# A norm without its subtraction, and two matmul groups moved by a slot, in a Mamba-and-attention kernel

## The chip, the cores and the metric

The kernel runs on one core of one Trainium2 chip. The metric is the device time of one execution in microseconds (us). Five engines matter: TensorE (PE, with its weight loads as PEld), VectorE (DVE), ScalarE (ACT), GpSimd (POOL) and SyncE (SP), whose queue issues nearly all DMAs. [...]

## The reference

The input x is 4 images of 512 channels and 64 x 64 positions (4096 positions in sequence). Two layers follow each other. `_gn` is a group norm over groups of 16 channels.

```python
def layer_norm(x, g, b):
    mu = jnp.mean(x, axis=-1, keepdims=True)
    var = jnp.mean((x - mu) ** 2, axis=-1, keepdims=True)
    return (x - mu) * lax.rsqrt(var + EPS) * g + b
...
def step(h, inp):                       # inside mamba()
    dt_t, B_t, C_t, x_t = inp
    dA = jnp.exp(dt_t[:, :, None] * A)
    h = dA * h + (dt_t * x_t)[:, :, None] * B_t[:, None, :]
    y = jnp.einsum('bds,bs->bd', h, C_t)
    return (h, y)
...
# layer 0, _L0_conv_ref
xn = layer_norm(xf, norm_g, norm_b)
chunks = xn.reshape(B, L, 4, D_MODEL).transpose(2, 0, 1, 3).reshape(4 * B, L, D_MODEL)
ym = mamba(chunks, in_proj_w, conv_w, conv_b, x_proj_w, dt_proj_w, dt_proj_b, A_log, D_param, out_proj_w)
ym = ym + skip_scale * chunks
y = ym.reshape(4, B, L, D_MODEL).transpose(1, 2, 0, 3).reshape(B, L, C)
y = layer_norm(y, norm_g, norm_b)
y = jnp.einsum('blc,oc->blo', y, proj_w) + proj_b
...
x = x + _L0_conv_ref(_gn(x), ...)       # layer 0
x = x + _L1_conv_ref(_gn(x), ...)       # layer 1: linear attention over the 4096 positions
```

`mamba` works on 128 channels with 256 inner channels and 16 states: an input projection, a causal convolution of 4 taps, Silu, projections to dt, B and C, softplus, the scan above, a gate by Silu(z) and an output projection.

## The kernel before, in words

Everything lies with channels on the partitions (128) and positions along the free axis. A tile is 512 positions of an image (32 tiles), a step is one chunk of 128 channels of a tile (c = 0 to 3, 128 steps), and a step is cut into 16 slots (`SLOTS`). A slot (`slot`, from L657) scans two times 128 rows x 512 positions, a row being a channel and a state: GpSimd makes `bx` = dt x B two slots ahead (`drive`, L655), ScalarE makes `dA` by Exp into PSUM three scans ahead (`decay`, L647), VectorE scans (L673). A product with C on VectorE follows (`product`, L696): it covers 384 of the 512 positions and reads C from PSUM, where a matmul `c_all` (`c_row`) has spread it; GpSimd takes the other 128 positions (L684). TensorE then sums the states into `y` (`fold_states`). `c_all` has a single PSUM buffer, holds C for two slots, and is emitted when the product of a pair's second slot has been emitted. The products usually come one slot late, in the middle of the next slot; after the slots in `AWAY = (3, 10)` this is changed, so that slots 4 and 11 hold two products with one scan between them and slots 5 and 12 hold none.

Around the scan, the rest of the work is emitted slot by slot by `after()`. Some of it has fixed slots:

- `take_y` (ScalarE) and `gate` (GpSimd, L720) at slots 0/8 and 1/9;
- `time_banks` (two matmuls `pt`) at slot 2, `time_steps` (two Softplus, each way a table load) at slot 3;
- `inputs`, the input projection and convolution of the step after next, as `front`: four pieces of two tap matmuls into `pc`, two matmuls `pz`, one piece at each of the slots 3, 5, 6, 7, 8, 9;
- `out_proj` (four small matmuls with `skd`, two with `w_op`, into `po`) of the step before at slot 4, `with_skip` (a ScalarE copy) at slot 6, after which `leave` is added if the step was a tile's last;
- `to_rows` (GpSimd's dt product L561, two DMAs) at slot 4, Silu (with two table loads) at slot 10, `mixers` (`pd`) from slot 12.

The rest comes from four queues of generators: `ahead` (the next tile's load, group norm and layer norm: `normed`), `late` (the finished tile's second layer norm and projection: `projected`, matmuls `pp`), `rest` (the attention of the previous image: `pq`, `pk`, `pr`) and `light` (the next image's statistics). A generator yields words for what may come next: "wide" for a VectorE instruction over 4 x 512 positions, "one ahead" and "two ahead" for the matmuls that prepare it, "free" and "more" for what may go at once. `may` says at which slots such a word is allowed; `limit` says how many PSUM work banks (3 in all) the queues may hold; `credit` is a budget of TensorE work per slot. `later(n, ...)` emits something n slots later.

A layer norm (`layer_norm`, L363) sums over channels with matmuls (`mu_sums`), copies the sums (L373), spreads the mean into a bank (`mu`), subtracts it from the tile with a wide VectorE instruction (L390), squares on ScalarE (L396), does the same again for the variance (`var_sums`, `var`), takes Ln and Exp (L403, L404) and multiplies with a second wide instruction (L410). Names with `_a` are the norm of `normed`, with `_b` that of `projected`.

Of the kernel before, what the change touches and what calls it, by code (L numbers as in the profile page):

```python
# [14 lines left out]
P = 128  # L15
T = 512
# [8 lines left out]
def kernel(  # L25
# [143 lines left out]
    for i in range(NC):  # L169
        nc.vector.memset(mean[i * LANE : i * LANE + 1, :], 1.0 / C)  # L170
    grp = const.tile([P, P // GROUP, GROUP], F32, tag="grp", name="grp")
    nc.gpsimd.memset(grp, 1.0 / GROUP)
# [133 lines left out]
    for c in range(NC):  # L306
        nc.vector.tensor_scalar(w_pr[:, c, :], w_pr[:, c, :], g_sb[:, c : c + 1], None, ALU.mult)


    def stats_tile(name):  # L310
# [47 lines left out]

    def layer_norm(v, name, gained):


        def means(parts, what, when):
            yield from room()  # L363
            sums = work_bank(f"{what}_sums_{name}")
            for c in range(NC):
                mm(
                    sums[c * LANE : (c + 1) * LANE, :], ones.to_broadcast([P, LANE]), parts[c],
                    start=True, stop=True, abreast=NC,
                )
            got = wk.tile([P, T], F32, tag="sq", name=f"{what}_got_{name}", bufs=4)  # L370

            def take():
                nc.scalar.copy(got, sums)  # L373
                free()

            copied = later(1, take)
            yield
            yield from until(copied)
            yield when
            yield from room(when)  # L380
            bank = work_bank(f"{what}_{name}")
            mm(bank, mean.to_broadcast([P, P]), got, start=True, stop=True)
            return bank

        while norming:
            yield "wait"
        norming.append(name)
        mu = yield from means([v[:, c, :] for c in range(NC)], "mu", "one ahead")
        yield "wide"
        nc.vector.tensor_tensor(v, v, bc(mu, NC), ALU.subtract)  # L390
        free()
        yield "free"
        sqs = []
        for c in range(NC):
            sqs.append(wk.tile([P, T], F32, tag="sq", name=f"sq_{name}_{c}", bufs=4))
            nc.scalar.activation(sqs[c], v[:, c, :], AF.Square)  # L396
            if c == 1:
                yield "free"
        var = yield from means(sqs, "var", "two ahead")
        rs = wk.tile([P, T], F32, tag="sq", name=f"rs_{name}", bufs=4)  # L400

        def root():
            nc.scalar.activation(rs, var, AF.Ln, bias=eps)  # L403
            nc.scalar.activation(var, rs, AF.Exp, scale=-0.5)  # L404

        rooted = later(1, root)
        yield
        yield from until(rooted)
        yield "wide"
        nc.vector.tensor_tensor(v, v, bc(var, NC), ALU.mult)  # L410
        free()
        norming.clear()
        yield
        if gained:
            for c in range(NC):
                nc.scalar.activation(
                    v[:, c, :], v[:, c, :], AF.Identity,
                    bias=b_sb[:, c : c + 1], scale=g_sb[:, c : c + 1],
                )
                if c % 2:  # L420
                    yield "free"

    def normed(xn, pad, prev_pad, b, t, norm):
# [9 lines left out]
        yield from group_norm(body, body, norm)  # L433
        yield from layer_norm(body, f"a_{b}_{t}", True)
        nc.gpsimd.tensor_copy(pad, xn[:, :, T : T + NTAP - 1])

    def projected(ym, stats, x1, b, t):

        nm = f"{b}_{t}"
        yield from layer_norm(ym, f"b_{nm}", False)  # L440
        while no_tile():
# [8 lines left out]
        for o in range(NC):  # L450
            yield from room()
            pp = work_bank(f"pp_{nm}_{o}")
            for c in range(NC):
# [4 lines left out]
                if c == 1:  # L458
                    yield "more"
            taken.append(later(1, lambda o=o, pp=pp: take(o, pp)))  # L460
            yield
# [571 lines left out]
    with tc.manual_schedule():  # L1033
        credit, seen, mix, held[0], held_x[0] = 0.0, work["mm"], iter(()), 0, 0
        for n, (b, t, c) in enumerate(steps):
# [10 lines left out]
            for s in range(SLOTS):  # L1046
                def after():
# [17 lines left out]
                    if s == 3 and nxt is not None:  # L1065
                        nc.scalar.preload_act_table_set("softplus")
                        time_steps(nxt, names[n + 1])
                        nc.scalar.preload_act_table_set("natural_log_exp_and_others")
                    if s == 6 and before is not None:
                        pb_, pt_, pc_ = steps[n - 1]  # L1070
                        with_skip(before, xn[pb_, pt_], pc_)
                        if pc_ == NC - 1:
                            add_to(late, leave(pb_, pt_))
                    if s in (3, 5, 6, 7, 8, 9):
                        next(front, None)
                    if s == 4 and nxt is not None:
                        to_rows(nxt, 0, names[n + 1])
                        to_rows(nxt, 1, names[n + 1])
                    if s == 4 and before is not None:
                        pb_, pt_, pc_ = steps[n - 1]  # L1080
                        out_proj(before, xn[pb_, pt_], pc_, names[n - 1])
# [7 lines left out]
                    if s >= 12:  # L1089
                        next(mix, None)  # L1090
                    may = [
                        what for k, what in ((0, "wide"), (1, "one ahead"), (2, "two ahead"))
                        if any(a - 2 * k <= s <= a - k for a in AWAY) or (k == 2 and s == SLOTS - 1)
                    ]
                    if light and light[0][1] == "wait" or s in AWAY and not any(
                        q and q[0][1] == "wide" for q in (ahead, late)
                    ):
                        one(light)

                    limit[0] = 1 if 0 < s < 6 else 2  # L1100
                    credit = min(credit + 3.5 - (work["mm"] - seen), 2.6)
                    busy = False
# [75 lines left out]
```

## Time and profile before

| | us |
|---|---|
| median of 3 executions | 8081.14 |
| lowest, highest | 8077.04, 8089.07 |
| profiled execution, its own time | 8087.92 |
| its span in the profile | 8086.2 |
| first scan starts, last scan ends | 120.3, 7611.9 |
| DVE, POOL, PE, ACT busy | 7113.0, 6890.3, 6471.4, 5514.5 |

The page is of one execution. Busy time is the sum over an engine's instructions; PE's is that of pipelined matmuls, and an fp32 matmul appears as two records. A line number is that of the kernel's source; all matmuls have the helper's line L124 and are told apart by the names of what they write and read (out<-in, buffer numbers left out). In lines of waits come the total in us, the number of times and the longest one.

### The profile page before, as it was taken

The numbers are of one execution on the slowest core, as the hardware profiler recorded it, in microseconds if no ns is written. First come the engines' busy times: TensorE is split into PE (matmuls) and PEld (weight loads), VectorE is DVE, ScalarE is ACT, GpSimd is POOL, SyncE is SP. The second block draws the span as 40 slices with busy tenths as digits, with TensorE's granted clock in tenths as the row PEclk, the third lists the DMA queues.
The fourth block names the chain that finished last, engine by engine and source line by source line (L and its number), as shares of the span: only waits on it lengthen the run. The fifth ranks groups of instructions, "written<-read, shape, count | busy, mean of one in ns | idle before, by whom it ended". The sixth has DMA issues, their size and how long they took to land.

```text
span 8086.2 us, 92449 instructions
## 1 busy us (share of the span) xinstructions
PE 6471.4 (80%) x24800; PEld 2115.5 (26%) x24800; DVE 7113.0 (88%) x6815; ACT 5514.5 (68%) x8289; POOL 6890.3 (85%) x4597
## 2 busy tenths in 40 slices
PE   5677777667788878888788888888788888888599
PEld 1111111112222222322222222332222222322144
DVE  5999999999999999899999999999999999998600
ACT  4667777777767777677776767667777777776421
POOL 4999999999989989899998989888999999889600
PEclk8787888788899989898899999899889999999699
DMA  5666666666666666676666666667666666676402
GB/s 160 166 166 160 156 147 153 157 157 166 167 167 156 162 153 156 168 188 176 169 155 164 166 165 155 155 171 187 163 158 160 156 157 152 150 194 176 110 32 89
DMA packets 829199, 1265.98 MB, mean 157 GB/s; under 512 B 183912, under 2 KB 317560, under 8 KB 816384
## 3 DMA queue, kind: packets, MB, share of 16 engines
q1 hardware_dynamic: 804736, 1222.32, 59.7%
q0 software_dynamic: 16896, 33.56, 2.4%
q10 hardware_dynamic: 7040, 4.20, 0.2%
q8 instruction: 194, 3.18, 0.2%
q14 instruction: 333, 2.73, 0.1%
HBM read 1052.78 MB, written 206.57 MB: 156 GB/s over the span
## 4 chain that ended last, share of the span: by engine, by line
DVE 22%; PE 19%; DMA 17%; POOL 14%; issue 10%; ACT 9%; SPq 8%; POOLq 0%; DVEq 0%; ACTq 0%
DVE h L673 14%; POOL bx L655 10%; DMA d_all<-d_rows 9%; DVE h L696 7%; PE pq L124 5%; SPq L622 5%; DMA b_all<-b_rows 4%; ACT dA L647 3%; PE pc L124 3%; PE pr L124 3%; SPq L572 3%; PE y L124 3%; POOL h L684 2%; PE pp L124 1%; DMA c_sb<-c_rows 1%
## 5 line engine op out<-in xcount | busy, mean ns | idle before, releaser
L655 POOL TENSOR_TENSOR bx<-d_all,b_all 128x1024 f32<-128x1024 f32 x2048 | 4817.4, 2371 | 66.9 <-DVE h L673 51.5
L673 DVE TENSOR_TENSOR_SCAN h<-dA,st,bx 128x512 f32<-128x512 f32 x3584 | 4420.5, 1267 | 80.6 <-ACT dA L647 75.4
L647 ACT ACTIVATE dA<-d_all,a_t 128x512 f32<-128x512 f32 x4096 | 2780.4, 688 | 1764.2 <-DVE h L673 1727.5
L696 DVE TENSOR_TENSOR h<-h,c_all 128x768 f32<-128x768 f32 x2048 | 1906.7, 931 | 307.5 <-PE c_all L124 298.2
L124 PE MATMUL y<-h,fold 128*32 128x512 f32 x8192 | 1280.6, 701 | 160.5 <-POOL h L684 156.1
L684 POOL TENSOR_TENSOR h<-h,c_sb 128x512 f32<-128x512 f32 x1024 | 1299.3, 1269 | 121.4 <-DMA c_sb<-c_rows 33.5
L124 PE MATMUL pc<-xn,w_cv 128*128 128x512 f32 x2048 | 1078.8, 662 | 178.2 <-DVE xn L410 116.7
L124 PE MATMUL c_all<-parts,sel 128*128 128x384 bf16 x1024 | 368.3, 360 | 1058.5 <-DVE h L696 1056.1
L124 PE MATMUL pq<-w_qk,xa 128*128 128x512 f32 x2048 | 990.7, 615 | 1.9 <-ACT xa L348 1.9
L673 DVE TENSOR_TENSOR_SCAN h<-dA,bx 128x512 f32<-128x512 f32 x512 | 601.2, 1206 | 58.8 <-ACT dA L647 54.6
L124 PEld LDWEIGHTS pc<-xn,w_cv 128*128 128x128 f32 x2048 | 395.9, 204 | 807.7 <-issue 445.6
L124 PEld LDWEIGHTS <-sel 128*128 128x128 bf16 x1280 | 127.5, 100 | 1724.4 <-DVE h L696 1495.6
L683 POOL COPY st<-h 128x4 f32<-128x4 f32 x1024 | 206.9, 202 | 425.2 <-DVE h L673 382.2
L124 PEld LDWEIGHTS pq<-w_qk,xa 128*128 128x128 f32 x2048 | 402.8, 199 | 468.7 <-issue 446.2
L124 PE MATMUL pr<-xb,m 128*128 128x512 f32 x1024 | 500.4, 626 | 24.8 <-DMA xb<-x 16.5
L124 PE MATMUL pp<-xn,w_pr 128*128 128x512 f32 x1024 | 487.6, 602 | 3.8 <-DVE xn L410 3.8
L124 PEld LDWEIGHTS y<-h,fold 128*32 128x32 f32 x8192 | 170.9, 114 | 743.6 <-issue 281.0
L124 PE MATMUL y<-xz,dg 32*32 32x512 f32 x2048 | 340.4, 741 | 0.0
L720 POOL TENSOR_TENSOR xz<-xz 128x512 f32<-128x512 f32 x256 | 325.4, 1271 | 2.7 <-ACT xz L717 2.7
L561 POOL TENSOR_TENSOR dt<-dt,xz 128x1024 f32<-128x1024 f32 x128 | 302.2, 2361 | 25.5 <-ACT dt L553 25.5
L124 PE MATMUL pd<-xz,w_xp 128*128 128x512 f32 x512 | 311.6, 740 | 7.8 <-ACT xz L987 7.8
L771 ACT ACTIVATE kq<-pq 128x512 f32<-128x512 f32 x256 | 150.6, 588 | 232.6 <-PE pq L124 230.5
(169 smaller groups left out, 6063.9 us busy)
## 6 DMA issues: line engine op xcount, KB each, us to landing
d_all<-d_rows SPq DMA_DIRECT2D x2048, 256.0 KB, 6.6
b_all<-b_rows SPq DMA_DIRECT2D x4096, 64.0 KB, 2.2
d_rows<-dt SPq DMA_DIRECT2D x256, 512.0 KB, 3.7
c_sb<-c_rows SPq DMA_DIRECT2D x4096, 16.0 KB, 1.9
xs<-in_x_dram SPq DMA_DIRECT2D x32, 1024.0 KB, 5.8
xn<-in_x_dram SPq DMA_DIRECT2D x32, 1024.0 KB, 5.7
xr<-in_x_dram POOLq DMA_DIRECT2D x32, 1024.0 KB, 11.2
x<-xr SPq DMA_DIRECT2D x32, 1024.0 KB, 4.3
```

What stands on the lines that cost most here:

```text
L124: nc.tensor.matmul(out_, lhsT, rhs, **how)
L561: nc.gpsimd.tensor_tensor(f["both"][:, 1], f["both"][:, 0], f["xz"][:, 0], ALU.mult)
L572: nc.sync.dma_start(d[k * BLK : (k + 1) * BLK, v], src)
L622: nc.sync.dma_start(dst[k * BLK : (k + 1) * BLK, :], rows_[q * KS + k, :].partition_broadcast(BLK))
L647: nc.scalar.activation(dAs[k], fs[n]["d_all", e][:, 0, j, :], AF.Exp, scale=a_t[:, e, j, q : q + 1])
L655: nc.gpsimd.tensor_tensor(bxs[g], fs[n]["d_all", e][:, 1, jj * 2 : jj * 2 + 2, :], bc(b_all[g // JJ], 2), ALU.mult)
L673: nc.vector.tensor_tensor_scan(h[:, j, :], dAs.pop(2 * g + i), bxs[g][:, i, :], 0.0 if t == 0 else st[:, c, e, q, j : j + 1], ALU.mult, AL ...
L683: nc.gpsimd.tensor_copy(st[:, c, e, q, :], h[:, :, T - 1])
L684: nc.gpsimd.tensor_tensor(h[:, :, CUT:], h[:, :, CUT:], bc(c_sb.pop(g // JJ), NJ), ALU.mult)
L696: nc.vector.tensor_tensor(own, own, bc(c_all[g // JJ], 2), ALU.mult)
L720: nc.gpsimd.tensor_tensor(f["xz"][:, 1, e, :], f["xz"][:, 1, e, :], f["xz"][:, 0, e, :], ALU.mult)
L771: nc.scalar.activation(qk[i], pq, AF.Relu)
```

## The change

The second layer norm (`_b`, in `projected`) no longer subtracts the mean. The columns of the projection's weights, already multiplied by the gain, are made to have mean zero over the input channels at the start, so the projection takes the mean out of its input by itself. The variance is computed as the mean of squares minus the squared mean: a ScalarE Square of the mean bank, and one more matmul with `minus_first` that accumulates into the variance's bank. Both squares are taken about `about`, a constant from the skip scale and the mean of the norm's bias. The first norm keeps its form. `out_proj` moves from slot 4 to slot 3, `with_skip` and `leave` from 6 to 5, the first convolution piece from slot 3 to slot 4. The words "wide", "one ahead" and "two ahead" count from slot 10 only; statistics may come at slot 3 always; `limit` is 0 in slots 1 to 3, 1 in slots 0 and 4, 2 from slot 5 on (before: 1 in slots 1 to 5, otherwise 2); the credit grows by 3.6 instead of 3.5 a slot. Copies of sums and of the projection's result come by `soon()`, which is two slots later in slots 5 to 11.

```diff
+    minus_first = const.tile([P, 1], F32, tag="minus_first", name="minus_first")
+    nc.vector.memset(minus_first, 0.0)
+    nc.vector.memset(minus_first[0:1, :], -1.0)
...
+    pw = work_bank("pw_mean")
+    for c in range(NC):
+        mm(pw, ones.to_broadcast([P, P]), w_pr[:, c, :], start=(c == 0), stop=(c == NC - 1))
+    for c in range(NC):
+        nc.vector.scalar_tensor_tensor(
+            w_pr[:, c, :], pw, -1.0 / C, w_pr[:, c, :], ALU.mult, ALU.add
+        )
+    pw = work_bank("pw_about")
...
+    about = const.tile([P, 1], F32, tag="about", name="about")
+    nc.vector.scalar_tensor_tensor(about, pw[:, 0:1], -1.0 / C, sk, ALU.mult, ALU.mult)
...
+    def layer_scale(v, name):
...
+        yield from room()
+        sums = work_bank(f"mu_sums_{name}")
+        sums_into(sums, [v[:, c, :] for c in range(NC)], range(NC))
+        mu = yield from mean_of(sums, f"mu_{name}", None)
+        mu2 = wk.tile([P, T], F32, tag="sq", name=f"mu2_{name}", bufs=4)
+
+        def square():
+            nc.scalar.activation(mu2, mu, AF.Square, bias=about)
+            free()
+
+        squared = later(soon(), square)
...
+        def part(c):
+            sqs[c] = wk.tile([P, T], F32, tag="sq", name=f"sq_{name}_{c}", bufs=4)
+            nc.scalar.activation(sqs[c], v[:, c, :], AF.Square, bias=about)
...
+        var = yield from mean_of(sums, f"var_{name}", "two ahead", False)
+        mm(var, minus_first.to_broadcast([P, P]), mu2, start=False, stop=True)
+        yield from over_deviation(v, var, name)
...
     def projected(ym, stats, x1, b, t):
...
-        yield from layer_norm(ym, f"b_{nm}", False)
+        yield from layer_scale(ym, f"b_{nm}")
...
-            taken.append(later(1, lambda o=o, pp=pp: take(o, pp)))
+            taken.append(later(soon(), lambda o=o, pp=pp: take(o, pp)))
...
-                    if s == 6 and before is not None:
+                    if s == 5 and before is not None:
...
-                    if s in (3, 5, 6, 7, 8, 9):
+                    if s in (4, 5, 6, 7, 8, 9):
                         next(front, None)
...
-                    if s == 4 and before is not None:
+                    if s == 3 and before is not None:
                         pb_, pt_, pc_ = steps[n - 1]
                         out_proj(before, xn[pb_, pt_], pc_, names[n - 1])
...
-                        if any(a - 2 * k <= s <= a - k for a in AWAY) or (k == 2 and s == SLOTS - 1)
+                        if AWAY[1] - 2 * k <= s <= AWAY[1] - k
...
-                    if light and light[0][1] == "wait" or s in AWAY and not any(
+                    if light and light[0][1] == "wait" or s == AWAY[0] or s == AWAY[1] and not any(
                         q and q[0][1] == "wide" for q in (ahead, late)
...
-                    limit[0] = 1 if 0 < s < 6 else 2
-                    credit = min(credit + 3.5 - (work["mm"] - seen), 2.6)
+                    limit[0] = 0 if 0 < s < 4 else 1 if s in (0, 4) else 2
+                    credit = min(credit + 3.6 - (work["mm"] - seen), 2.6)
```

`sums_into`, `mean_of` and `over_deviation` hold what was inside `layer_norm`, and both norms call them.

## The prediction

> **What bounds the kernel now.** I read the page first, then each batch's stretch in the view of busy times by window, then DVE's waits, then the timelines of DVE and PE around one of those waits. The page gives the ranking, with DVE ahead of POOL:
>
> ```profile
> PE 6471.4 (80%) x24800; PEld 2115.5 (26%) x24800; DVE 7113.0 (88%) x6815; ACT 5514.5 (68%) x8289; POOL 6890.3 (85%) x4597
> DVE  5999999999999999899999999999999999998600
> ```
>
> The slot loop runs from the first scan at 120.3 us to the last at 7611.9 us. In windows cut at the batches (32 steps each), then the end after the loop:
>
> ```profile
> core 0: us, PE busy (x) PEld busy (x) DVE busy (x) ACT busy (x) POOL busy (x), PEclk, DMA share, GB/s
> 120.30:1920.60 1800.30, 1267.01 (x4666) 340.57 (x4666) 1744.36 (x1620) 1286.09 (x1905) 1711.50 (x1141) 0.81 0.66 159
> 1920.60:3823.00 1902.40, 1584.95 (x6192) 523.45 (x6192) 1777.10 (x1695) 1374.12 (x2072) 1724.19 (x1148) 0.91 0.66 166
> 7611.90:8086.20 474.30, 435.61 (x1508) 199.20 (x1508) 26.29 (x74) 102.80 (x166) 5.59 (x6) 0.92 0.17 58
> ```
>
> Batch 0 leaves DVE idle for 56 us of 1800; each later batch, which carries the attention of the one before, for 122 to 139 of 1890 to 1902. Together DVE stands idle for about 442 us of the loop's 7491.5. DVE's waits name the causes:
>
> ```profile
> DVE h L696 <- PE c_all L124: 298.2, 165, 6.0
> DVE kq L778 <- PE pk L124: 242.4, 42, 7.6
> DVE h L673 <- ACT dA L647: 130.1, 64, 46.7
> ```
>
> The kq wait lies almost wholly after the loop (9.8 us inside it) and 46.7 us of the dA wait before the first scan. Counting scans in the DVE timeline (two to a slot) sorts the rest: of the c_all wait 208 us fall in slot 4, 52 in slot 7, 18 in slot 15, 11 in slot 9; of the dA wait 62 in slot 12 and 19 in slot 5. The slot-4 wait in step 41, on DVE and then PE:
>
> ```profile
> 2458.61 2.25 DVE L410 TENSOR_TENSOR xn<-xn,var_a 128x2048 f32<-128x2048 f32 x1
> 2460.79 1.27 DVE L673 TENSOR_TENSOR_SCAN h<-dA,st,bx 128x512 f32<-128x512 f32 x1
> 2461.98 0.92 DVE L696 TENSOR_TENSOR h<-h,c_all 128x768 f32<-128x768 f32 x1
> 2462.83 1.27 DVE L673 TENSOR_TENSOR_SCAN h<-dA,st,bx 128x512 f32<-128x512 f32 x1
> 2465.73 0.95 DVE L696 TENSOR_TENSOR h<-h,c_all 128x768 f32<-128x768 f32 x1 [1.63 <-PE c_all L124]
> ```
>
> ```profile
> 2456.59 1.41 PE L124 MATMUL pt<-dt,w_dt 32*128 32x512 f32 x4
> 2460.92 2.47 PE L124 MATMUL pc<-xn,w_cv 128*128 128x512 f32 x4 [2.92 <-DVE xn L410]
> 2463.32 1.94 PE L124 MATMUL mu_sums_b<-xn,ones 128*32 128x512 f32 x8
> 2465.19 0.50 PE L124 MATMUL c_all<-parts,sel 128*128 128x384 bf16 x1
> ```
>
> In slot 4 the second product follows the first after one scan, so the c_all between them has 1.2 us. PE comes late: the slot-3 taps (pc) got the bank that the variance still held, waited 2.92 us for the wide multiply on DVE, and c_all stood behind them.
>
> **What the Trainium skill says.** (1) "PSUM — Partial Sum Buffer", Engine vs sequencer instructions: matmuls start and complete in program order. The fence above agrees: c_all's product input was ready at 2462.9, it started at 2465.19. (2) "VectorE: DVE Perf Modes", The perf-mode tier table: an fp32 tensor_tensor of 2048 columns takes 2293 ns, with a PSUM operand no faster. The trace has 2267 for L390. (3) "ScalarE: Activation LUTs", What ACT_TABLE_LOAD costs: a load is about 1283 ns, and a pointer bias adds 93 ns to an activation. The trace has 1283, and 614 for the Square without bias.
>
> **The change, part by part.** A matmul record costs PE 0.44 us in a row (the chain of waits ends with 256 pr records in 112.69 us); an fp32 matmul is two records. The instruction orders of both programs give counts and slots.
>
> *Subtraction removed.* 32 wide L390 instructions on mu_b at 2.267 us: 31 in the loop, one after it. DVE is the bound, and nothing hides them: 31 x 2.267 = **-70**.
>
> *Added for it.* ACT: 32 Squares of the mean (about 0.71 us with bias) and 93 ns more on each of 128 squares, 35 us on an engine idle 28% of the loop; it counts only in slots 3 and 10, where the order puts only a handful of them. PE: one more matmul a tile, 0.88 us in slots 5 to 7, counted with c_all below. Setup: four matmuls (3.5 us), four DVE passes of 512 columns (0.67 each by the bn_stats row L739, 2.7 in all) and the tiny *about*. DVE waits for x there, but the passes stand ahead of bn_stats that free x's buffers: between 0 and 6; **+2**. After the loop a 2.27 us pass gives way to a Square (0.71) and a matmul (0.88): **-1**, between -2 and +1.
>
> *Moves.* Slot 3 now emits out_proj, slot 4 the first taps; no new bank is taken in slots 1 to 3; wide steps stand at slot 10 (and var_a at slot 7) instead of 3 and 10. None of the moved steps issues a DMA; SP's and POOL's instructions and counts stay. Between the c_all of slots 2 and 4, PE's list shrinks to y (1.06 + 1.07 by the timeline), pt (1.41) and po (1.06 + 4 x 0.44): 6.4 us in every step, where before it held taps and often another 1 to 4 us, plus the wait for the bank. From the end of slot 1's product to slot 4's second DVE needs five scans (1.18 apart) and two products (0.85): 7.6 us. c_all itself takes 0.4. 6.8 against 7.6: the wait goes, but with only 0.8 to spare. po waits for gate on POOL, which ends about 2.9 us into slot 2, while PE reaches po's second half after 6: hidden. I leave 15 of the 208: **-193**.
>
> What is late next. Slots 4 and 5 now hold both tap pieces (3.5 us) and the background matmuls banned from slots 1 to 3. PE has about 8.6 us there (7.8 before, since c_all was late); 23 steps hold 9 us or more. Summing the excess, and scaling by what the same sum gave of slot 7's wait before (40 for 52): 33, **-19**. Slot 9: two steps reach 12, 11 becomes 15, **+4**. Slots 12 and 13 hold about 9.6 us in some 20 steps, where 8 to 9 was usual: 18 becomes 48, **+30**.
>
> ACT next. After slot 3's second scan it does dA, a table load, two Softplus, a table load, dA: 0.69 + 1.28 + 1.27 + 1.28 + 0.69, ready at 5.3 us. DVE without wide step or wait needs that dA at 5.4. Today's slot-4 wait hides anything more. In the fourth of steps with two group_norm pieces (0.80 each) ACT is ready at 6.7 to 6.9: 31 instead of 19, **+12**. At slot 10, Silu and loads make it 6.5; steps without a wide step wait 1.0. Steps c = 1 lose their cover and c = 2 gain it: **+5**.
>
> POOL next: bx was waited for 7 us. POOL is busy for 1712 to 1724 us a batch, and slot 4 gives it the dt product (2.36) besides. Between 0 and 60; the wait in slot 4 was its rest too: **+18**.
>
> Sum: -70 + 2 - 1 - 193 - 19 + 4 + 30 + 12 + 5 + 18 = **-212**. The profiled execution took 8087.9 (span 8086.2 and 1.7 around it), so 7876 on that scale; the median of the runs, 8081.1, is 6.8 lower: **7869**.
>
> **Rivals.** *The wait moves to ACT.* If nearly every step's dA in slot 5 comes 1.3 us late (two extra activations each time) then 166 instead of 31: **8004**. For it: ACT's 5.3 stands a hair below DVE's 5.4. Against: slot 3 is now empty of other activations in three steps of four. *POOL becomes the bound.* With the batches at 1800 us, as batch 0 with POOL 95% busy, the loop would be 7200: **7789**, hence no worse; but if half the dt product came onto the path in every step (128 x 1.18 = 151), **8002**. bx was ready 2 us or more ahead in most slots, which speaks against. *The bank ban bunches PE's work, and it ends slower.* The attention's matmuls come four to a bank, 3.5 us. If a bank's worth falls ahead of c_all(6) or c_all(14) and wholly on the path in four steps of five, 0.8 x 128 x 3.5 = 358 is lost: 8081 - 212 + 358 = **8227**. It decides from 1.7 us lost a step (212/128). For it: 86 of the steps pass 7 us in slots 4 and 5, where 68 did. Against: only 23 pass 9. *Larger gain*: if slots 9, 15 and bx don't grow and slot 7 vanishes, another 85: **7784**. That the subtraction only seems to go I exclude: the order holds no such instruction on mu_b.
>
> **Numbers.** The main case 0.68, its own range 7805 to 7935; the larger gain 0.09; ACT or POOL taking more of it 0.15; bunching to a slower kernel 0.06, to no change 0.02. No change means within 0.2%, 16 us, about what this measurement can tell. Range 7785 to 7985. Faster 0.92, same 0.02, slower 0.06.
>
> **What would show it.** DVE's busy time falls by about 72; no L390-like row on mu_b. The c_all wait falls from 298 to about 120, almost none of it in slot 4 and the most in slots 15 and 7. No pc waits for DVE's wide multiply. The dA wait stays near 145 in all. Batches 1 to 3 fall to about 1840 us, batch 0 to about 1770; the end stays at 474. Wrong would be: a slot-4 wait that survives, a dA wait above 250, a bx wait above 80, or an end longer by an attention left over (the order says none is).

## The result and the profile after

The changed kernel takes **8140.6 us** (median of 4 executions, 8134.4 to 8152.4) against 8083.1 (8077.0 to 8089.1) for the kernel before, run beside it: a ratio of 1.0073, interval 1.0055 to 1.0090. It is slower, where the forecast was 7869 and at most 7985. The profiled execution took 8134.4 (span 8132.7). In its page, the rows of engines and of slices that were shown of before:

```profile
PE 6532.7 (80%) x24880; PEld 2120.7 (26%) x24880; DVE 7062.6 (87%) x6790; ACT 5521.9 (68%) x8321; POOL 6882.5 (85%) x4597
DVE  5999999999999999988999899998999999988600
```

DVE is busy for 50 us less and still the span is 46.5 us longer. (The page's busy time is no sum over instructions: a stretch in which two of them overlap counts once. So the forecast's fall of 72 is met by the sum of the durations, -71 in the table below, and not by the busy time.) The windows, cut again at the batches and at the last scan, say where (the stretch before the first scan grew from 120.3 to 122.8):

```profile
core 0: us, PE busy (x) PEld busy (x) DVE busy (x) ACT busy (x) POOL busy (x), PEclk, DMA share, GB/s
122.80:1940.50 1817.70, 1281.97 (x4680) 344.44 (x4680) 1732.58 (x1614) 1282.11 (x1906) 1711.02 (x1142) 0.82 0.65 157
1940.50:3854.20 1913.70, 1590.85 (x6208) 520.07 (x6208) 1766.15 (x1686) 1375.97 (x2080) 1723.14 (x1148) 0.91 0.67 165
7666.00:8132.70 466.70, 429.32 (x1510) 195.68 (x1510) 23.94 (x74) 103.83 (x167) 5.59 (x6) 0.94 0.18 59
```

Every batch is longer, the first too (1818 against 1800), although DVE is busy 12 us less in it. So the loss lies in the loop, 7491.5 to 7543.2, and it is idle time of DVE. Its waits:

```profile
DVE h L763 <- PE c_all L124: 281.0, 221, 8.6
DVE kq L845 <- PE pk L124: 247.6, 40, 7.6
DVE h L740 <- ACT dA L714: 186.5, 111, 46.7
DVE h L740 <- POOL bx L722: 41.4, 55, 2.9
```

(L763 is the product, L740 the scan; they were L696 and L673.) The c_all wait has hardly shrunk, but it now comes 221 times instead of 165; the dA wait has grown from 64 times to 111; bx, which was below the rows shown, is there with 55 waits. Sorted by slot as before, over the loop (idle of more than 60 ns, us):

| | before | after | what was predicted of the difference | difference |
|---|---|---|---|---|
| sum of DVE's durations | 7538 | 7467 | -70 | -71 |
| c_all in slot 4 | 212 | 101 | -193 | -111 |
| c_all in slots 7, 9, 11, 15 | 52, 11, 0, 18 | 67, 20, 28, 68 | -19 + 4 + 0 + 30 = +15 | +101 |
| c_all in other slots | 9 | 5 | 0 | -4 |
| dA in slot 5 | 19 | 23 | +12 | +4 |
| dA in slot 12 | 63 | 66 | +5 | +3 |
| dA in slots 14 and 15 | 1 | 50 | 0 | +49 |
| bx | 7 | 42 | +18 | +35 |
| everything else waited for | 40 | 65 | 0 | +25 |
| overlap lost | | | 0 | +19 |

The last row needs a word. Two DVE instructions that follow each other without a stall overlap in the records by 0.080 us (2458.61 + 2.25 is 2460.86, and the next one in the fence of the prediction starts at 2460.79). There were 339 stalls in the loop before and 524 after, so fewer instructions follow at once: 6078 overlaps, 488.3 us, before, and 5831, 469.2 us, after. The rows add up to +50, with small dA and gap terms to the +51.7 of the loop. The rows of c_all count all idle time ahead of the product; in slot 4 that includes gaps of 0.1 us which DVE's own scan ends, 4 us of the 212 and 6 of the 101.

**The wait that was to vanish.** The forecast rested on step 41, so here is step 41 of the changed kernel, PE and then DVE:

```profile
2482.47 0.50 PE L124 MATMUL c_all<-parts,sel 128*128 128x384 bf16 x1 [3.63 <-DVE h L763]
2482.91 1.93 PE L124 MATMUL y<-xz,dg 32*32 32x512 f32 x8
2484.76 1.93 PE L124 MATMUL y<-h,fold 128*32 128x512 f32 x8
2486.63 2.08 PE L124 MATMUL pt<-dt,w_dt 32*128 32x512 f32 x4
2488.64 1.93 PE L124 MATMUL po<-xn,skd 32*32 32x512 f32 x8
2490.49 2.70 PE L124 MATMUL po<-xz,w_op 128*128 128x512 f32 x4
2493.03 0.33 PE L124 MATMUL c_all<-parts,sel 128*128 128x384 bf16 x1
```

```profile
2489.11 0.92 DVE L763 TENSOR_TENSOR h<-h,c_all 128x768 f32<-128x768 f32 x1
2489.95 1.27 DVE L740 TENSOR_TENSOR_SCAN h<-dA,st,bx 128x512 f32<-128x512 f32 x1
2493.39 0.95 DVE L763 TENSOR_TENSOR h<-h,c_all 128x768 f32<-128x768 f32 x1 [2.17 <-PE c_all L124]
```

The list between the two c_all is exactly the predicted one: y, pt, po, no taps and no wait for DVE's multiply. But each group of eight records takes 1.93 us, not 1.06; the list takes 10.3 us (2482.91 to 2493.19), not 6.4, and DVE stands for 2.17 us. In the view of windows TensorE's granted clock is 1.00 until 2474.9 us, 0.50 from there to 2491.97, which is some way into po, and then 1.00 again. So the clock had fallen before the list began; the records ahead of the list are slow already:

```profile
2476.05 0.50 PE L124 MATMUL c_all<-parts,sel 128*128 128x384 bf16 x1 [3.60 <-DVE h L763]
2476.48 1.93 PE L124 MATMUL y<-h,fold 128*32 128x512 f32 x8
2478.34 0.50 PE L124 MATMUL pd<-parts,minus 128*128 128x384 bf16 x1
```

The clock fell in the idle stretch of 3.60 us ahead of them, their 2.79 us of work didn't bring it back, a second idle stretch of 3.63 us followed, and then it took 9.5 us of work (2482.47 to 2491.97). The Trainium skill names this: "TensorE: Matmul & The Clock Gate", HAM oscillation — how this bites in real kernels, gives as a rule that idle gaps of TensorE above about 3.4 us throttle its clock again, so that the next matmuls start cold. The trace agrees in kind, not in the figure: here the clock fell 2.5 us into the gap (2472.44 to 2474.9), and of the 3.4 us before that TensorE had worked for 0.58. Over all steps, TensorE idled 3.53 us on average ahead of the c_all of slot 2 where the y group that folds the states then took over 1.4 us, and 1.46 us where it didn't; po ends between 6.28 us (5th percentile) and 10.72 (95th) after c_all starts, with a median of 7.87; the product is due at about 7.6.

### The profile page after: what moved, and what is told of

Its sections match the earlier page's. It is cut to its first block, busy times and chain, and to the rows that moved or that the text cites. A ratio compares the mean times of both kernels' runs of the same rounds, so it can differ in the third digit from the quotient of the medians.

```text
span 8132.7 us, 92670 instructions
## 1 busy us (share of the span) xinstructions
PE 6532.7 (80%) x24880; PEld 2120.7 (26%) x24880; DVE 7062.6 (87%) x6790; ACT 5521.9 (68%) x8321; POOL 6882.5 (85%) x4597
## 4 chain that ended last, share of the span: by engine, by line
DMA 23%; PE 21%; POOL 16%; DVE 13%; SPq 10%; issue 9%; ACT 8%; POOLq 0%; DVEq 0%; ACTq 0%
DMA d_all<-d_rows 12%; POOL bx L722 11%; DVE h L740 8%; SPq L689 6%; PE pq L124 5%; DVE h L763 4%; PE y L124 4%; SPq L639 3%; ACT dA L714 3%; DMA b_all<-b_rows 3%; DMA c_sb<-c_rows 3%; PE pp L124 3%; POOL h L751 2%; PE pc L124 2%; PE pr L124 2%
## 5 line engine op out<-in xcount | busy, mean ns | idle before, releaser
L740 DVE TENSOR_TENSOR_SCAN h<-dA,st,bx 128x512 f32<-128x512 f32 x3584 | 4425.9, 1267 | 164.0 <-ACT dA L714 127.9
L763 DVE TENSOR_TENSOR h<-h,c_all 128x768 f32<-128x768 f32 x2048 | 1908.1, 932 | 292.9 <-PE c_all L124 281.0
L124 PE MATMUL y<-h,fold 128*32 128x512 f32 x8192 | 1297.5, 710 | 277.8 <-POOL h L751 271.1
L124 PE MATMUL pc<-xn,w_cv 128*128 128x512 f32 x2048 | 1000.1, 620 | 4.6 <-ACT xn L443 4.6
L740 DVE TENSOR_TENSOR_SCAN h<-dA,bx 128x512 f32<-128x512 f32 x512 | 602.4, 1207 | 72.3 <-ACT dA L714 58.6
L124 PEld LDWEIGHTS pc<-xn,w_cv 128*128 128x128 f32 x2048 | 375.3, 194 | 602.6 <-issue 463.4
L124 PE MATMUL pp<-xn,w_pr 128*128 128x512 f32 x1024 | 507.6, 628 | 6.5 <-DVE xn L414 3.8
L124 PE MATMUL pz<-xn,w_z 128*128 128x512 f32 x512 | 282.9, 646 | 47.7 <-ACT got_mu_b L391 30.2
```

The source lines that it names most:

```text
L124: nc.tensor.matmul(out_, lhsT, rhs, **how)
L740: nc.vector.tensor_tensor_scan(h[:, j, :], dAs.pop(2 * g + i), bxs[g][:, i, :], 0.0 if t == 0 else st[:, c, e, q, j : j + 1], ALU.mult, AL ...
L763: nc.vector.tensor_tensor(own, own, bc(c_all[g // JJ], 2), ALU.mult)
```

## The experiments

Ratios are to the kernel before, measured beside each run on the same chip; the intervals are of 95%. All waits are of the profiled execution, in us, and sorted by slot as above. The columns leave out c_all in slots 1 and 3.

| | median us | ratio (interval) | c_all slot 4 | slots 7, 9, 11, 15 | dA | bx |
|---|---|---|---|---|---|---|
| before | | 1 | 212 | 82 | 84 | 7 |
| after | 8140.6 | 1.0073 (1.0055, 1.0090) | 101 | 183 | 140 | 42 |
| e1 norm only | 8078.5 | 0.9987 (0.9981, 0.9994) | 201 | 85 | 145 | 7 |
| e2 moves of slots only | 8164.8 | 1.0098 (1.0083, 1.0113) | 281 | 105 | 76 | 4 |
| e3 after, old limit | 8229.4 | 1.0177 (1.0162, 1.0192) | 369 | 102 | 137 | 7 |
| e4 after, old words | 8134.6 | 1.0058 (1.0042, 1.0075) | 153 | 168 | 145 | 21 |
| e5 after, extra records | 8081.4 | 0.9996 (0.9988, 1.0005) | 31 | 197 | 137 | 56 |
| e6 after, y earlier | 8137.7 | 1.0068 (1.0051, 1.0085) | 93 | 185 | 139 | 44 |
| e7 e1, y earlier | 8150.9 | 1.0082 (1.0065, 1.0098) | 225 | 137 | 129 | 7 |
| e8 after, late sums | 8131.6 | 1.0059 (1.0044, 1.0074) | 99 | 203 | 108 | 44 |
| e9 before, extra records | 8131.5 | 1.0057 (1.0042, 1.0072) | 175 | 139 | 67 | 10 |
| e10 e1, extra records | 8081.7 | 0.9996 (0.9987, 1.0004) | 191 | 141 | 103 | 10 |
| e11 e5 and e8 together | 8067.5 | 0.9976 (0.9970, 0.9983) | 28 | 204 | 111 | 66 |
| e12 e5, slot 1 only | 8107.4 | 1.0024 (1.0014, 1.0034) | 30 | 208 | 145 | 55 |
| e13 e9, slot 1 only | 8124.4 | 1.0042 (1.0028, 1.0057) | 188 | 88 | 91 | 10 |
| e14 e10, slot 1 only | 8083.3 | 1.0000 (0.9993, 1.0006) | 184 | 90 | 152 | 10 |
| e15 e11, slot 1 only | 8104.8 | 1.0025 (1.0015, 1.0036) | 27 | 216 | 121 | 78 |

### Which part costs: e1 to e4

**e1** keeps the new norm and puts back the old slots, words, limit and credit:

```diff
-                    if s == 5 and before is not None:
+                    if s == 6 and before is not None:
...
-                    if s in (4, 5, 6, 7, 8, 9):
+                    if s in (3, 5, 6, 7, 8, 9):
...
-                    if s == 3 and before is not None:
+                    if s == 4 and before is not None:
...
-                        if AWAY[1] - 2 * k <= s <= AWAY[1] - k
+                        if any(a - 2 * k <= s <= a - k for a in AWAY) or (k == 2 and s == SLOTS - 1)
...
-                    if light and light[0][1] == "wait" or s == AWAY[0] or s == AWAY[1] and not any(
+                    if light and light[0][1] == "wait" or s in AWAY and not any(
...
-                    limit[0] = 0 if 0 < s < 4 else 1 if s in (0, 4) else 2
-                    credit = min(credit + 3.6 - (work["mm"] - seen), 2.6)
+                    limit[0] = 1 if 0 < s < 6 else 2
+                    credit = min(credit + 3.5 - (work["mm"] - seen), 2.6)
```

> The new second norm with the slot table, limit, words and credit of before. Theory S (the new slot table costs more than the norm saves): the 31 wide passes leave DVE and nothing else moves, so 8000 to 8030 us; the c_all wait in slot 4 stays near 210 us and the c_all waits in slots 11 and 15 stay at 0 and about 20. Theory N (the new norm itself brings the waits, by its longer chain on ScalarE and its later variance): 8085 us or more, with c_all waits of over 50 us in slot 15 and dA waits in slots 14 and 15 as in the changed kernel (50 us).

Measured: 8078.5 us, 0.13% under the kernel before. The profiled execution was one of its faster ones (span 8055.3), and in it the loop is 27 us shorter. The durations of DVE's instructions fall by 68 us, as worked out, but the waits grow by 34 and 7 us of overlap are lost. Its dA row (before: 130.1, 64 times):

```profile
DVE h L740 <- ACT dA L714: 190.8, 99, 46.6
```

Of the dA wait, 120 us now fall in slot 12, before 63. A wide pass of 2.27 us at slot 10 had covered the stretch in which ScalarE does Silu with its two table loads and dA comes late. With the pass gone DVE waits there about 1.25 us in a step of c = 1 (0 to 40 us) and of c = 2 (20 to 40 us). So more than half of what the norm saves comes back one slot later, at the engine that it had hidden.

**e2** moves `out_proj` to slot 3, `with_skip` and `leave` to slot 5 and the taps to slots 4 to 9 in the kernel before, and nothing else:

```diff
-                    if s == 6 and before is not None:
+                    if s == 5 and before is not None:
...
-                    if s in (3, 5, 6, 7, 8, 9):
+                    if s in (4, 5, 6, 7, 8, 9):
...
-                    if s == 4 and before is not None:
+                    if s == 3 and before is not None:
```

> The kernel before with out_proj at slot 3, with_skip and leave at slot 5 and the first taps at slot 4, nothing else. Theory S says that the move alone gains little, because the wide pass at slot 3 now keeps out_proj's bank waiting as it kept the taps': the c_all wait in slot 4 stays over 150 us, that of slot 7 falls from 52 to below 20 (PE's list in slots 4 and 5 is a microsecond shorter), and the time is 8040 to 8090 us. Theory N says the move does what it is meant to: the slot-4 wait falls to 100 us as in the changed kernel, and the time to 7960 to 8000 us.

Measured: 8164.8 us, 1% slower, slot 4 up from 212 to 281 us. PE's waits show that the bank wait only changed its owner; the row of pc (116.7 us before) is gone, and there is

```profile
PE po L124 <- DVE xn L410: 105.3, 62, 3.2
```

**e3** is the changed kernel with the old limit, **e4** with the old words for wide steps and statistics:

```diff
-                    limit[0] = 0 if 0 < s < 4 else 1 if s in (0, 4) else 2
+                    limit[0] = 1 if 0 < s < 6 else 2
```

```diff
-                        if AWAY[1] - 2 * k <= s <= AWAY[1] - k
+                        if any(a - 2 * k <= s <= a - k for a in AWAY) or (k == 2 and s == SLOTS - 1)
...
-                    if light and light[0][1] == "wait" or s == AWAY[0] or s == AWAY[1] and not any(
+                    if light and light[0][1] == "wait" or s in AWAY and not any(
```

> The changed kernel with the bank limit of before (1 in slots 1 to 5, otherwise 2). Theory S with the bank ban as its cause: the steps with over 9 us of TensorE work in slots 4 and 5 fall from 23 to none, the c_all wait in slot 7 from 67 us to below 25, that of slot 11 from 28 to below 10; but slots 2 and 3 get 35 steps over 9 us, and the wait in slot 4 rises from 101 to some 180. 8060 to 8120 us. Theory N: the limit is not what matters, 8130 to 8150 us.

> The changed kernel with the places of wide, one ahead and two ahead, and of the statistics, as before: the variance's pass of the finished tile is at slot 3 of c = 2 again, seven slots earlier, so that the projection no longer falls into slots 12 to 15. Theory S with the late variance as its cause: the c_all wait in slot 15 falls from 68 us to about 20, the dA waits in slots 14 and 15 from 50 to below 10, while the slot-4 wait stays near 100 or rises to 150 (out_proj's bank waits for the wide pass in 61 steps): 8040 to 8100 us. Theory N: 8130 to 8150 us, the waits stay where they are.

Measured: e3 8229.4, e4 8134.6. The bank ban in slots 1 to 3 is worth 268 us in slot 4 (369 to 101), and a part of that is taken again in later slots: slot 7 goes from 6 to 67, slot 11 from 4 to 28, bx from 7 to 42. This is the bunching of the rivals, in slot 7: in the changed kernel each of the 56 steps that wait there for over 0.15 us has about 9.0 us of PE work between two c_all, 3.7 of it both tap pieces and 4.2 background matmuls (pq, pp, pr, sums). Before, 36 steps waited. In slot 11 pz waits for a bank whose sums ScalarE has not yet copied, a row of PE's waits that the kernel before doesn't have:

```profile
PE pz L124 <- ACT got_mu_b L391: 30.2, 14, 2.9
```

e4 brings slot 15 back from 68 to 18: with the new words the projection falls into slots 12 to 15 of c = 2, and a step that waits in slot 15 has 4.3 us of pp ahead of c_all; in e4 it has 1.7, before 0.3. The dA wait in slots 14 and 15 goes with it, from 50 us to almost none. But slots 4, 7 and 9 take 153, 94 and 50 instead of 101, 67 and 20, dA in slot 12 takes 116 instead of 66, and the time is that of the changed kernel within the intervals. The larger credit was tried in no run of its own.

### TensorE's pace: e5 to e7

**e5** adds 32 matmul records a step of the form y <- xz,dg in slots 1 and 9 (16 each, not the 32 each of the expectation), into the bank that y uses next. Their results are written over. What the lists of slots 2 and 3 hold doesn't change.

```diff
-            ys[n, e] = ps_y.tile([P, T], F32, tag="y", name=f"y_{n}_{e}")
...
+    def warm_y(f, n, e):
+        ys[n, e] = ps_y.tile([P, T], F32, tag="y", name=f"y_{n}_{e}")
+        for _ in range(2):
+            for k in range(P // BLK):
+                r = slice(k * BLK, (k + 1) * BLK)
+                mm(ys[n, e][r, :], dg[r, e, :], f["xz"][r, 0, e, :], abreast=P // BLK, start=True, stop=True)
+        work["mm"] -= 2
...
+                    if s % (SLOTS // 2) == 1:
+                        warm_y(f, n, s // (SLOTS // 2))
```

> The changed kernel with 32 more matmul records in each of slots 1 and 9: the dg-by-xz matmuls of y are issued twice more, ahead of their usual place, which stays (they start the sum anew, so nothing is added). PE's list between the c_all of slots 2 and 4 is unchanged. Theory C (what is left of the wait in slot 4 is TensorE at half clock after its idle stretch): the share of y groups in slot 3 that take 1.9 us instead of 1.07 falls from 64% to below 30%, and the slot-4 wait from 101 us to below 50, although TensorE has more to do; slot 9 or 11 may lose 10 to 20. 8080 to 8130 us. Rival L (the list of slots 2 and 3 is simply too long): the slot-4 wait stays at 100 us or grows, 8140 to 8170 us.

Measured: 8081.4 us, 0.7% under the changed kernel, with 4,096 records of useless work. Step 41, PE:

```profile
2486.90 0.32 PE L124 MATMUL c_all<-parts,sel 128*128 128x384 bf16 x1 [0.43 <-DVE h L763]
2487.16 1.06 PE L124 MATMUL y<-xz,dg 32*32 32x512 f32 x8
2488.15 1.06 PE L124 MATMUL y<-h,fold 128*32 128x512 f32 x8
2489.14 1.13 PE L124 MATMUL pt<-dt,w_dt 32*128 32x512 f32 x4
2490.20 1.06 PE L124 MATMUL po<-xn,skd 32*32 32x512 f32 x8
2491.19 1.98 PE L124 MATMUL po<-xz,w_op 128*128 128x512 f32 x4
```

The idle time ahead is 0.43 us instead of 3.63, the granted clock is 1.00 over the list instead of 0.50, the same five groups take 6.0 us instead of 10.3, and po's median end is 6.27 us after c_all starts: the forecast's 6.4. Of the y groups that fold the states in slot 3, 64% took over 1.4 us after the change; here 3%. The mean granted clock rises from 0.889 to 0.924, and the wait in slot 4 falls from 101 to 31 us, of which 11 are gaps of 0.1 us that DVE's own scan ends. So the order of the forecast was right, its pace was not. Yet even with 181 of the 193 us gained in slot 4 the kernel is only as fast as before: what fails besides is the rest of the sum.

**e6** moves the y <- xz,dg matmuls themselves to slots 1 and 9 in the changed kernel, without repeating them, and **e7** does so in e1:

```diff
-        if q == 0:
-            ys[n, e] = ps_y.tile([P, T], F32, tag="y", name=f"y_{n}_{e}")
-            diagonal(ys[n, e], dg[:, e, :], fs[n]["xz"][:, 0, e, :])
...
+                    if s % (SLOTS // 2) == 1:
+                        open_y(f, n, s // (SLOTS // 2))
```

> The changed kernel with the dg-by-xz matmuls of y moved from slot 2 (and 10), where they stand between the two c_all, to slots 1 and 9. The list of slots 2 and 3 loses 1.06 us at full clock, 2 us at half clock. Both C and L expect the slot-4 wait to fall from 101 us to below 30, and the time to 8040 to 8075 us if nothing else takes its place. If it takes its place (theory R: every microsecond that one wait gives back is asked for by the next, on ScalarE in slot 5 and on GpSimd), the dA and bx waits grow by more than half of it and the time stays above 8100 us.

> The new norm with the old slot table (run e1) and the early dg-by-xz matmuls. There the wait in slot 4 (200 us) has three parts: the wide pass at slot 3 that holds the bank of the taps in c = 1 and 2, the list, and the clock. If list and clock are half of it, the wait falls to 90 to 120 us and the time to 7985 to 8030 us; if the held bank is nearly all of it, the wait stays above 170 us and the time at 8060 to 8080 us. Theory R expects under half of what the wait loses to reach the end.

Measured: e6 8137.7, the same as the changed kernel; e7 8150.9, 0.9% over e1. Slot 4 keeps 93 of 101 us in e6, although its list is a group shorter. The median end of po falls from 7.87 to 5.29 us after c_all starts, but a quarter of the steps still end after 9.07 us (8.55 in the changed kernel), and these make the wait. Of the 35 steps whose po ends after 9 us, 34 have a group that folds the states in over 1.4 us; of all steps it is 35%, and 3% in e5. So what holds c_all there is again the pace, and not the number of groups. In e7 slot 4 even rises from 201 to 225, and the time is above all that was expected; why stays open.

### ScalarE in slots 14 and 15: e8

The 49 us of dA wait in slots 14 and 15 stand beside two rows of ScalarE's waits:

```profile
ACT sum L561 <- DMA out_dram<-res: 39.0, 7, 9.2
ACT sum L561 <- DMA xr<-in_x_dram: 28.6, 15, 9.5
```

(Before, the first row isn't there and the second is one wait of 9.3 us, after the loop; after, 19.1 us of it in 14 waits lie in the loop.) The statistics of the next layer (`sum`) read a tile that a transfer brings (`xr`) and write their unused output into the buffers from which `res` is sent out. While ScalarE stands before a sum, the dA behind it isn't made: of the 50 us, 30 follow a sum that waited for the store and 7 one that waited for xr. **e8** gives them other buffers and lets them come two slots later:

```diff
-        yield from pause(4)
+        yield from pause(6)
...
-                unused = wk.tile([P, T], F32, tag="res", name=f"{v}_{nm}_{o}", bufs=2)
+                unused = wk.tile([P, T], F32, tag="sq", name=f"{v}_{nm}_{o}", bufs=4)
```

> The changed kernel with the sums of the projected tile two slots later after its transfer (6 slots of pause instead of 4) and with their unused output in another ring of buffers than that of the stored results. Theory A (the dA waits in slots 14 and 15 come from ScalarE standing before these sums, which wait for the transfer xr, 14.0 us to land where it was 11.2, and for the store out<-res): these waits fall from 50 us to below 10, and the time to 8085 to 8110 us. Rival: they come from other work that stands on ScalarE there (the copies of pp and pd), and stay above 35 us; 8130 to 8145 us.

Measured: 8131.6 us. In the loop both rows are gone, and the dA wait in slots 14 and 15 falls from 50 to 7 us: that the sums make it is shown. How much of it the buffers give and how much the two slots isn't, since both came in one run. But slot 15's c_all takes 85 instead of 68, slot 5's dA 30 instead of 23, and 9 of the 43 us reach the end, which the intervals hardly tell apart from none.

### The same extra records in both orders: e9 to e15

**e9** is the kernel before, **e10** e1, each with e5's extra records; **e11** is e8 with them.

> The kernel before with the same 32 extra dg x xz matmul records in slots 1 and 9 as e5 (their results are written over). If TensorE's half-clock stretch after idle slots is a cost of both kernels alike, the slow share of y groups in slot 3 falls from 53% to under 10%, the wait for c_all in slot 4 falls from 212 us by about as much as in e5 (70 us, to about 140), and the kernel takes about 8020 us (0.992). Then the change's own loss (0.7%) is apart from the clock: changed plus extra matmuls at 8081 would be 0.7% to 0.8% over this one. Rival: the half-clock stretch is something the change brought (slot 3 64% slow instead of 53%); then the extra records give the kernel before next to nothing, 8075 to 8095, and the clock explains the whole loss.

> The new norm with the old slots, words and limits (e1, 8078.5 us) plus the same 32 extra records. If the parts add: 60 us below e1, 8015 to 8025 us, ratio about 0.992, and faster than both kernels by over 0.5%; slot 4 c_all from 201 to about 130, dA in slot 12 still near 120. If e1's gain was only slack in the same chain, it equals the kernel before with the extra records within 0.1%. If the ACT waits for dA are next in line, it gains less than 30 us (over 8050) and slot 12 dA grows.

> The changed kernel with the extra records (e5, 8081.4 us) and with the sums' pause 6 and their unused output in another pool tag (e8). If the two losses are independent (half clock in slots 2 and 3; ACT held by sums that wait for a transfer in slots 14 and 15), the gains add: 8081 less 9 = 8072, dA in slots 14 and 15 near 0. If in e8 the gain was lost because slot 15's wait for c_all took its place behind a slow TensorE, more of it comes through with the faster one: 8040 to 8055, c_all in slot 15 under 60. If it is a bunching that goes round whatever is taken out, 8078 to 8085.

Measured: 8131.5, 8081.7, 8067.5. The first is outside all that was expected; the second has the time of its last case, but not its sign, since dA in slot 12 falls (120 to 71 us). In the old order the records make the kernel before slower by 0.6% and leave e1 where it was. Slow groups in slot 3 vanish there as well (53% to 4%), but slot 4 keeps 175 of 212 us and 191 of 201, since the taps still wait for the bank that DVE's wide multiply reads (PE's row of pc behind xn is 140.5 and 143.1 us, 116.7 before); and slot 11, which the records of slot 9 delay, takes 57 and 63 us instead of 0 and 2. Slot 3 is held up too: its wait for c_all, which now stands behind the records of slot 1, is 16 and 18 us instead of 1.5; in e5 it is 5. With the extra records in both orders the changed kernel is the faster one: e5 has a ratio of 0.9996 and e9 one of 1.0057. That is no gain on the kernel before as it stands. e11's gains add up (8081 less 9 was to give 8072), and it is the fastest kernel of this study, 0.24% under the kernel before. Its DVE waits:

```profile
DVE h L763 <- PE c_all L124: 227.3, 197, 6.6
DVE h L740 <- ACT dA L714: 157.8, 101, 48.0
DVE h L740 <- POOL bx L722: 64.7, 74, 3.3
```

**e12** to **e15** leave out the records of slot 9: e5, e9, e10 and e11 with those of slot 1 alone.

```diff
...
-                    if s % (SLOTS // 2) == 1:
-                        warm_y(f, n, s // (SLOTS // 2))
+                    if s == 1:
+                        warm_y(f, n, 0)
...
```

> The changed kernel with the 16 extra records of slot 1 alone (none in slot 9). If slot 1's records give the whole gain of e5 and slot 9's only cost TensorE time ahead of slot 11, slot 4's c_all is again about 31 us, slots 9 and 11 go back from 36 and 42 towards 20 and 28, and the time is below e5's 8081: 8040 to 8065. If e5's gain was luck of the schedule, 8100 to 8150, or a gain that no wait accounts for.

> The kernel before with the 16 extra records of slot 1 alone. If slot 9's records were what cost e9 its 45 us (slot 11's c_all 0 to 57), slot 11 is back under 10 us, slot 4 stays near 175 (before 212), and the time is 8045 to 8075. If the extra work costs in any slot, 8100 or more. In both cases slot 4 stays over 150, since there the wait is not for TensorE's clock: out_proj stands behind it.

> The new norm on the old slots (e1, 8078.5) with the 16 extra records of slot 1 alone. As e13: slot 11 back under 15 us from e10's 63, slot 4 near 190, 8040 to 8070. If this equals e1 within 0.2%, the old slot order gains nothing from the clock at all.

> e11 (changed kernel, late sums, extra records; 8067.5 us) without slot 9's records: c_all of slots 9 and 11 (43 and 39 us) go down by 20 to 40 together, slot 4 under 35, dA in slots 14 and 15 near 0: 8030 to 8050, the fastest so far. If the waits only go round, 8060 to 8075.

Measured: 8107.4, 8124.4, 8083.3, 8104.8, all four outside what I expected for the likelier theory; for e12 to e14 it is the alternative that holds, for e15 neither. The waits moved as described: slot 4 stays at 30 and 27 in the new order, and slot 11 is back at 0 and 2 in the old one. But the times did not follow. In the changed kernel slot 1's records take 71 us off slot 4 and 33 off the time; those of slot 9 are worth another 26 (slot 15 at 59 us instead of 84, dA in slot 12 at 59 instead of 69), so they were no mere cost. The sums' edit, worth 14 us in e11 over e5, is worth 3 in e15 over e12. In the kernel before, slot 1's records cost 40 us by the medians and 28 in the profiled execution. Its loop is 26 us longer, 18 of it waits, 5 lost overlap and 3 durations: what slot 4 gives (24 us) slot 3 takes (22 us for c_all instead of 1.5), and slots 9 and 15, dA, bx and others grow by some 25. Why all these grow stays open, and with it how much of e5's gain over e9 is the pace and how much the fit of one schedule.

## Why the prediction was wrong

**Right.** The 31 passes: DVE's durations fell by 71, 70 was said. The setup: the first scan comes 2.5 us later, 2 was said. The order of the list in slots 2 and 3, no more pc behind DVE's multiply, and c = 1 losing its cover in slot 12 while c = 2 gains it (0 to 35 and 20 to 0 us). The end after the loop changed by -8, not -1; it is -8 in e1, with the norm alone, and -1 in e2, with the moves of slots alone, but -1 again in e8 and e12; the reason is open. Of the four signs that were to show the forecast wrong, one came: the wait in slot 4 that survives.

**The step that failed first: "6.8 against 7.6: the wait goes, but with only 0.8 to spare".** The 6.8 was summed from durations of one step whose y groups took 1.06 us. In the trace of the kernel before, 53% of the fold groups in slot 3 took over 1.4 us, so the slow pace was there to be seen. The change also lets TensorE idle longer ahead of that list (the ban leaves slots 1 to 3 without background matmuls), the median idle time ahead of the c_all of slot 2 goes from 2.13 to 3.11 us, and the share of slow groups rises to 64%. With the ban lifted (e3) the two are 1.38 us and 46%. With the fast pace (e5) the same term measures 31 us instead of 101, against the 15 left in the forecast, so the pace is what was left out of it. This is 82 us of the 259 between the predicted sum, -212, and the measured difference of the spans, +46.5.

**The second: what is late next.** For slots 7, 9, 11 and 15 together +15 was said, and it is +101. The terms for slots 7 and 9 counted PE's work and scaled it with the old wait; slot 11, where a bank waits for ScalarE's copy, had no term, and slot 15 took 68 instead of 48. e3 shows that the ban drives slots 7 and 11, e4 that the words drive slot 15. That is 86 us.

**The third: ScalarE and GpSimd.** dA in slots 14 and 15, where the statistics hold ScalarE behind transfers (e8) once the new words have put them there (e4), had no term: 49 us. bx grew by 35 instead of 18. The guess that the wait in slot 4 was POOL's rest fits the table: where slot 4 waits over 170 us bx is 4 to 10, at 153 it is 21, at 93 to 101 it is 42 to 44, at 27 to 31 it is 55 to 78. No run changed GpSimd's work alone, so this is a pattern and not a proof. Other waits grew by 25, and 19 of overlap went with the more numerous stalls.

**The rivals.** The one given 0.06, bunching by the bank ban, had the sign, and one of its two places: DVE waits for c_all(6) in slot 7, and in slot 11 besides. The wait for c_all(14), in slot 15, is there too, but not by the ban: without it slot 15 keeps 76 us (e3), and the old words bring it back to 18 (e4). The rival didn't need the 358 us put down for it: 101 in these slots together were enough, because the gain that they stood against was nearly halved by the pace and eaten into by the other two engines. The rivals of ScalarE and GpSimd were each there in part. I treated them as alternatives; they came together.

**Where the gain of each part went.** The norm alone saves 68 us of DVE and keeps 27 in the loop of its profile (e1), 9 by the medians. The moves, with limit, words and credit, add 0.86% on top of e1 by the ratios, some 70 us, and nothing with the extra records in both (e10 and e5, 8081.7 and 8081.4). So the new norm is worth having in the old order, and the moves are not, unless TensorE is kept busy ahead of slot 2 and ScalarE free of the transfer, as in e11, which is 0.1% under e1 by the ratios. That rests on one schedule: with slot 1's records alone (e15, 8104.8) it is slower than the new norm in the old order with them (e14, 8083.3). No run has e1 with the sums' edit.

## What to carry to other kernels

Where a wait is to vanish by less than a microsecond, take the distribution of the durations in that very slot over all steps, not the durations of one step: at the low clock the same groups took 1.93 us instead of 1.06, and banning background matmuls from the slots ahead made TensorE idle longer there and the slow steps more frequent. A wait or a wide pass on the bounding engine is at the same time slack for every other engine, so price its removal by asking each of them what it does in that time; here more than half of what e1, e8 and e12 gained in one place was asked for again elsewhere, though in e5 most of it reached the end. Judge the parts of such a change one by one, since one was worth keeping (e1) and the sum was not.

## What the runs showed of the hardware that I had not expected

Useless matmuls made a kernel faster: 32 more records a step took 0.7% off (e5 against the changed kernel), and in the slot-4 list the groups ahead of c_all then took 1.06 us instead of 1.93. The same records in another order made it slower by 0.6% (e9). TensorE's clock falls without a whole window of idleness: of the 240 falls to 0.50 in the changed kernel's loop 117 came while a matmul record was running, and at the median TensorE had been busy for a quarter of the 3.4 us before. And every stall of DVE costs 0.080 us more than its idle time shows, since instructions that follow at once overlap by that much in the records.
